# Giving each piece of a software-pipelined round its own place in the order, in a two-layer graph and attention kernel

## The chip, the cores and the metric

The kernel runs on one core of a Trainium2 chip. The metric is the device time of one execution in microseconds (us). A core has a matmul engine (TensorE, PE in profiles), a vector engine (VectorE, DVE), an activation engine (ScalarE, ACT), a general engine (GpSimd, POOL) and a synchronisation engine (SyncE, SP), which here only issues transfers. Each engine takes its instructions in the order in which the program emitted them, and semaphores hold an instruction until the data or the buffer that it needs is there.

## The reference

Inputs are `x` of 128 graphs x 128 nodes x 512 features, one 128 x 128 adjacency `adj` for all, and the weights, all float32. Two layers follow each other:

```
q, k, v = x @ Wq0.T, x @ Wk0.T, x @ Wv0.T            # layer 0
rel = adj.T * (q @ k.T)                              # per graph, 128 x 128
x   = layernorm(x + (rel / norm(rel, axis=rows)) @ v)

q, k, v = x @ Wq1 + bq, x @ Wk1 + bk, x @ Wv1 + bv   # layer 1, 8 heads of 64
w   = softmax(q @ k.T / 8 + where(adj == 0, -1e9, 0))
x   = layernorm(x + w @ v)
```

## The kernel before

**Groups and kinds of projection.** The 128 graphs go in 32 groups `g` of 4. A group needs five projections, each a product of a 512 x 512 weight with 512 tokens: `m` (layer 0, with Wq0 and Wk0 multiplied together once at the start, so that one projection takes the place of two), `v0`, and in layer 1 `q`, `k`, `v1`. Each is done by Strassen's scheme in its variant with few additions: seven products of quarters in place of eight. Three of the seven (1, 6, 7) are done whole (`whole`); the other four (2 to 5) are each split again by the same scheme (`inner`), two for either half of the tokens, and their seven small products are added up in pairs. Sums of weight blocks are made once at the start; sums of token blocks are made in each group by `token_sums` and `inner_token_sums` (L271 to L311), mostly on POOL.

**Pieces.** A `Projection` is cut into pieces that are emitted one at a time. `inner(th, n)`, for two token halves `th` and `n` of 0 to 3, runs small matmuls (L446) into PSUM tiles `c` and `d`, and ACT and DVE carry them out: n = 0 a copy on ACT (L458) and an add on DVE (L459), n = 1 two copies (L464, L465), n = 2 an add (L470), n = 3 a copy (L474) and, for `th` = 1, a sum of two halves on POOL (L476). `whole(i, m)` for i of 1, 6, 7 and m of 0, 1 runs four matmul instructions (L436) into one half of a PSUM tile `a`, which is never cleared between i = 1, 6 and 7: each product is added to what is there. `add` (L483, L488, L491) reads `a` on DVE after 1 and after 6, so product 6 can't start in that half before DVE has read product 1, and product 7 not before it has read product 6. The read after 6 also needs the POOL sum of L476.

**Other pieces of a group.** In layer 0 `l0_score` does the 128 x 128 products of a graph (L542), masks them on DVE (L543) and squares them on POOL (L544); `l0_norm` sums the squares of all four graphs by a matmul (L553); `l0_out` multiplies by `v0` and adds to `x`. `x1_spill`, `x1_stage` and `x1_transpose` bring the result through DRAM into a transposed form, with its token sums; `x_transpose` does so for `x` itself. In layer 1 `attn_scores` does eight heads of a graph, masked on DVE (L130), `attn_exp` two heads' exponentials on ACT (L627), `attn_spill` writes them to DRAM (L634), `attn_stage` and `attn_transpose` fetch and transpose them (L642, L646), `attn_out` multiplies by `v1` (L659), and `attn_back`, `attn_rows`, `attn_res`, `attn_sum`, `attn_stats`, `attn_norm`, `attn_write` bring the rows back, add the residual, normalise and store.

**Shared buffers.** Most tiles have one buffer. The tile tagged `v0` holds the v0 projection of one group and, once that is used, the softmax weights of graphs 0 and 1 of an earlier group; `yT` likewise serves m, the weights of graphs 2 and 3, and the residual rows of graphs 0 and 1. PSUM has a pool of six tiles (`ps_m`) for all but the `a` tiles, which have two (`ps_a`). Streamed weights (`stream`, L193) have a ring of two.

**The order.** It is written by hand. Round r holds the projections m and v0 of group r + 1 and q, k, v1 of group r, in five slots of 7 units, so a round is R = 35 units long. Every piece has a key, and pieces are emitted by rising key. The matmul pieces of a projection sit at fixed offsets in its slot, the same for each kind: for instance (L831 and the line after it)

```
    WHOLES = ((4.17, 1, 0), (5.33, 1, 1), (6.5, 6, 0), (7.67, 6, 1), (8.83, 7, 0), (10.0, 7, 1))
    INNER = ((0, 0, 0), (1.17, 0, 1), (2.33, 0, 2), (3.5, 0, 3), (2.4, 1, 0), (3.57, 1, 1), (4.67, 1, 2), (5.83, 1, 3))
```

where an entry is (offset, i, m) or (offset, th, n). The other pieces have keys from small tables: `ZERO` for layer 0, `STEADY` for the attention of most groups, `QUICK` for the last but one and `LAST` for the last. Pieces may share a key; then the order of the calls decides. A lower-layer group is thus two rounds ahead of the attention that still drains.

Of the kernel before, what the change touches and what calls it, by code (L numbers as in the profile page):

```python
# [18 lines left out]
def kernel(  # L19
# [15 lines left out]
    nc = tc.nc  # L35
# [3 lines left out]
    G = 4  # L39
# [338 lines left out]
    class Projection:  # L378
# [10 lines left out]

        def begin(self):  # L390
            k, g = self.kind, self.g
            self.xT, self.t, u = (XT[g], TX[g], UX) if k in ("m", "v0") else (X1T[g], TX1[g], UX1)
            self.u = u.get(g)
            self.y = {}
            if k == "m":
                YT[g] = y = one.tile([P, C, G, P], F32, tag="yT", name=f"yT_{g}")
            elif k == "q":
                QT[g] = y = one.tile([P, C, G, P], F32, tag="qT" if g < NG - 1 else "yT", name=f"qT_{g}")
            elif k == "k":
                KT[g] = y = one.tile([P, C, G, P], F32, tag="kT", name=f"kT_{g}")  # L400
            elif k == "v0" or not self.late:
                y = one.tile([P, G, D], F32, tag="v0", name=f"{k}_{g}")
                (V0 if k == "v0" else V1)[g] = self.y = {h: y[:, 2 * h:2 * h + 2] for h in range(2)}
            else:
                V1[g] = self.y = {0: one.tile([P, 2, D], F32, tag="v10", name=f"v1_{g}_0")}
                self.s = one.tile([P, 2, 2, HF], F32, tag="rel", name=f"s_{self.name}")
            if not self.wide:
                self.y = {h: y[:, :, 2 * h:2 * h + 2] for h in range(2)}

        def out(self, eh, th):  # L410

# [264 lines left out]
        nc.sync.dma_start(o, OD.pop((g, b)).rearrange("p f d -> p (f d)"))  # L676
        SOFT[g, b] = o, SOFT[g, b][1]

    def attn_res(g, b):
        xr = room(g, b, 1)  # L680
        nc.sync.dma_start(xr, X1D[g, b // 2][b % 2])
        SOFT[g, b] = SOFT[g, b][0], xr, SOFT[g, b][1]

    def attn_sum(g, b):

        o, xr, rs = SOFT[g, b]
        f = o.rearrange("p (f r) -> p f r", r=Q)
        nc.vector.tensor_tensor(f, f, rs.rearrange("p s y a -> p (s y a)")[:, :, None].to_broadcast([P, A * H // 2, Q]),
                                op=ALU.mult)
# [103 lines left out]
    def last_store(g, b):  # L793
# [4 lines left out]


    R = 35  # L800
    dense, short = {}, {}

    ZERO = (
        ((18, 19, 20, 21), 22, (36, 36, 37, 37), 38, (39, 40), (40, 41), (42, 43), (46, 47, 49, 49)),
        ((11.5, 11.5, 11.75, 12.5), 13.75, (19.5, 21.5, 22.5, 18.5), 23.5, (26, 28), (29, 29.5), (30, 31.5), (37.5, 38.5, 41, 44.5)),
        ((11.5, 12.5, 11.75, 12.5), 13.75, (18.5, 19.5, 21, 22), 23, (24, 25), (25, 26), (26, 28), (31, 32, 33, 34)),
    )
    STEADY = (  # L810
        (32.75, (32.5, 34.5, 35, 35, 35), (35, 36.5), 41.5, (44, 49, 51.5, 56, 60, 64.5, 68, 68)),
        (32.75, (35.5, 38.5, 38.5, 41.5, 41.5), (41.5, 41.5), 42, (47.5, 49, 51, 52, 60, 65, 69, 69)),
        (49, (49.5, 49.5, 50.5, 50.5, 52.5), (55, 55), 57.5, (58.5, 67.75, 67.75, 70, 73, 75, 77, 77)),
        (49, (50.5, 55, 55, 55, 55), (56.5, 56.5), 60.5, (63.5, 67.75, 69, 74.5, 76, 82, 83, 85.5)),
    )
    QUICK = (
        (32.75, (32, 33.5, 34.5, 34.5, 35), (35, 38), 40.5, (41, 43, 43.5, 47.5, 48.5, 50.5, 50.5, 50.5)),
        (36, (37, 37, 37, 37, 37), (39.5, 40.5), 41.5, (44.5, 45.5, 47.5, 50, 52, 53, 55, 62)),
        (37, (37.5, 41, 41, 41, 41), (41, 41), 45.5, (47.5, 50, 57.5, 57.5, 57.5, 59, 59.5, 63)),
        (37, (39, 41.5, 42.5, 44, 47), (44, 47), 49.5, (51, 52, 57.5, 61, 61, 64.5, 68.5, 68.5)),  # L820
    )
    LAST = (
        (18, (18, 18), (20, 22), (25.25, 25.5), 29, 35, 37.5),
        (18, (18, 19.5), (24, 24.5), (28, 31), 40, 45.5, 46),
        (19.5, (20, 23.5), (28.5, 29), (31, 37), 41, 51, 51),
        (23, (23.5, 27), (29.5, 32), (33.5, 41.5), 51, 53, 54.5),
    )


    PLAIN = ((0, 1), (1, 5), (3, 6), (4, 2), (5, 3), (6, 7), (9, 4))  # L830
    WHOLES = ((4.17, 1, 0), (5.33, 1, 1), (6.5, 6, 0), (7.67, 6, 1), (8.83, 7, 0), (10.0, 7, 1))  # L831
    INNER = ((0, 0, 0), (1.17, 0, 1), (2.33, 0, 2), (3.5, 0, 3), (2.4, 1, 0), (3.57, 1, 1), (4.67, 1, 2), (5.83, 1, 3))

    RES = 59

    def at(r, k, f, *a):
        short.setdefault(R * r + k, []).append((f, a))

    for r in range(-1, NG):
        todo = [("m", r + 1), ("v0", r + 1)] if r < NG - 1 else []  # L840
        if r < 0:
            todo.reverse()
        todo += [("q", r), ("k", r), ("v1", r)]
        for j, (kind, g) in enumerate(todo):
            if not 0 <= g < NG:
                continue
            pr = Projection(kind, g)
            if pr.plain:
                for k, i in PLAIN:
                    dense[R * r + 7 * j + k] = pr.step, (i,)  # L850
                continue
            for k, f, *a in (*((k, pr.whole, i, m) for k, i, m in WHOLES), *((k, pr.inner, th, n) for k, th, n in INNER)):
                assert R * r + 7 * j + k not in dense
                dense[R * r + 7 * j + k] = f, a
            if g or kind not in ("m", "v0"):
                if not (g == 1 and kind in ("m", "v0")):
                    at(r, 7 * j - 7.5, stream, kind, g)
    halves = [(dh, h) for dh in range(2) for h in range(2)]
    for g in range(NG):

        for h in range(2):
            if g:
                at(g - 2, 12, load_staged, g, h)
                at(g - 1, 12 + 4 * h, load, g, h)
        last = g == NG - 1

        sc, no, ou, de, ln, sp, st, tr = ZERO[0 if g == 0 else 2 if last else 1]
        for h in range(2):
            at(g - 1, sp[h], x1_spill, g, h)
            at(g - 1, st[h], x1_stage, g, h)  # L870
        for i, (dh, h) in enumerate(halves):
            if g or i:
                at(g - 2, ((25.5, 27, 28.5, 30) if g != 1 else (22, 23, 24, 25))[i], x_transpose, g, dh, h)
            at(g - 1, tr[i], x1_transpose, g, dh, h)
        for b in range(G):
            at(g - 1, sc[b], l0_score, g, b)
            at(g - 1, ou[b], l0_out, g, b)
            at(g - 1, ln[b // 2], l0_layernorm, g, b)
        at(g - 1, no, l0_norm, g)
        at(g - 1, de, l0_rstd, g)  # L880

        if last:
            at(g, 2, last_residual, g)
        for b in range(G):
            if last:
                sc, e, t, o, st, no, w = LAST[b]
                at(g, sc, last_scores, g, b)
                for i in range(2):
                    at(g, e[i], last_exp, g, b, i)
                    at(g, t[i], last_transpose, g, b, i)  # L890
                    at(g, o[i], last_out, g, b, i)
                at(g, st, last_stats, g, b)
                at(g, no, last_norm, g, b)
                at(g, w, last_store, g, b)
                continue
            s, ex, sp, st, pk = QUICK[b] if g == NG - 2 else STEADY[b]
            at(g, s, attn_scores, g, b)
            for i in range(4):
                at(g, ex[i + 1], attn_exp, g, b, 2 * i)
            for i in range(2):  # L900
                at(g, sp[i], attn_spill, g, b, i)
            at(g, st, attn_stage, g, b)
            pieces = attn_transpose, attn_out, attn_back, attn_rows, attn_sum, attn_stats, attn_norm, attn_write
            for k, f in zip(pk, pieces):
                at(g, k, f, g, b)
                if f is attn_rows:
                    at(g, RES if g < NG - 2 and b < 2 else k, attn_res, g, b)

    at(-1, 8, masks)
    V1S = ((one, "v10"), (one, "v11"))  # L910
    WTS = ((one, "wl"), (two, "wT"))
    at(-1, 41, layer1_weights, "k", "k", V1S)
    at(-1, 41, streamed_sums, "k", nc.gpsimd)
    for k, name, eng in ((38.5, "v0", nc.vector), (17, "m", nc.vector), (28, "q", nc.gpsimd), (49.5, "k", nc.gpsimd),
                         (52, "v1", nc.gpsimd)):
        at(-1, k, resident_sums, name, eng)
        if name in ("m", "v0"):
            at(-1, k, streamed_sums, name, eng)

    with tc.manual_schedule():  # L920
        layer0_weights()
        for k in sorted({*short, *dense}):
            if k == -R:
                weight_sums(whole_weights("m"), m21, nc.vector)
                for name, key, stage in (("v", "v1", V1S), ("q", "q", WTS)):
                    layer1_weights(name, key, stage)
                    streamed_sums(key, nc.gpsimd)
            for f, a in short.get(k, ()):
                f(*a)
            if k in dense:  # L930
                f, a = dense[k]
                f(*a)


# [27 lines left out]
```

## Time and profile before

Three runs took 3173.1, 3183.88 and 3184.35 us; the median is 3183.88. The profiled execution spans 3181.8 us.

| engine | busy us | share of the span |
|---|---|---|
| PE (matmuls) | 2638.7 | 83% |
| PEld (weight loads, beside the matmuls) | 2262.9 | 71% |
| DVE | 1927.3 | 61% |
| POOL | 1467.6 | 46% |
| ACT | 1020.3 | 32% |

The mean granted clock of TensorE is 0.933. The queues moved 553 MB, 174 GB/s over the span, and the transfers kept the DMA engines busy for 60% of it. Between the first and the last 100 us the profile repeats itself every 99 us or so, once per group. A row of waits names the waiting instruction, its engine and line, then what it waited for, the sum in us, how many times, and the longest. A row of a stretch gives its bounds and length, then the busy time of each engine with the number of its instructions.

### The profile page before, as it was taken

What the parts mean: (1) busy time and instruction counts of PE and PEld (TensorE: products, weight loads), DVE (VectorE), ACT (ScalarE), POOL (GpSimd) and SP (SyncE); (2) the same over time, 40 slices, a digit from 0 to 9 for tenths busy, and PEclk for the clock granted to TensorE, in tenths of its full rate; (3) what the DMA queues carried; (4) which work ended last, traced back from release to release, by engine and by line L of the source; (5) the groups of instructions that cost most, each with busy time, mean ns of one, the idle gap of its engine ahead of it and who ended that gap; (6) DMA issues with size and microseconds to landing.
All of it is one profiled execution on the core that took longest, in us unless ns stands there. A gap on an engine that the chain in (4) does not pass through costs nothing. (4 is left out here: it accounts for less than half of the span.)

```text
span 3181.8 us, 54401 instructions
## 1 busy us (share of the span) xinstructions
PE 2638.7 (83%) x18456; PEld 2262.9 (71%) x18456; DVE 1927.3 (61%) x5440; ACT 1020.3 (32%) x3598; POOL 1467.6 (46%) x1958
## 2 busy tenths in 40 slices
PE   7888888888888888888888888888888888888887
PEld 5677677777777677677767777777767767776776
DVE  5555566656666556665566665566655666555666
ACT  1233333233332333333323323233233333332334
POOL 5534544445444345444454443545434544445444
PEclk9999999999999999999999999899999999999999
DMA  6555666666656666656666665665565665666654
GB/s 158 152 152 168 193 181 174 176 173 178 188 168 172 177 171 186 189 159 174 174 186 185 179 172 170 173 190 174 166 176 169 187 189 160 181 171 182 185 171 127
DMA packets 532248, 553.29 MB, mean 174 GB/s; under 512 B 40192, under 2 KB 427392, under 8 KB 531968
## 3 DMA queue, kind: packets, MB, share of 16 engines
q1 hardware_dynamic: 531968, 549.81, 60.4%
q8 instruction: 145, 2.38, 0.3%
q14 instruction: 135, 1.11, 0.1%
HBM read 380.44 MB, written 169.21 MB: 173 GB/s over the span
## 5 line engine op out<-in xcount | busy, mean ns | idle before, releaser
L627 ACT ACTIVATE w<-w,nmax 128x128 f32<-128x128 f32 x992 | 384.8, 392 | 3.9 <-DVE nmax L130 3.9
L436 PE MATMUL pa_v<-wc_v,tx 128*128 128x256 f32 x1024 | 270.4, 387 | 61.6 <-DVE v L491 61.5
L446 PE MATMUL pc_v<-wd_v,ux 128*128 128x128 f32 x756 | 176.0, 320 | 144.4 <-ACT v L458 144.4
L476 POOL TENSOR_TENSOR qT<-qT 128x512 f32<-128x512 f32 x32 | 40.6, 1269 | 523.0 <-ACT qT L474 523.0
L446 PEld LDWEIGHTS pc_v<-wd_v,ux 128*128 128x128 f32 x756 | 143.6, 223 | 174.6 <-ACT v L458 156.4
L130 DVE CUSTOM_DVE_ANT_0 w<-ps,mask 128x128 f32<-128x128 f32 x1024 | 221.4, 286 | 32.7 <-PE ps L607 31.1
L436 PEld LDWEIGHTS pa_v<-wc_v,tx 128*128 128x128 f32 x1024 | 175.3, 191 | 87.7 <-DVE v L491 73.8
L436 PE MATMUL pa_m<-tx,wc_m 128*128 128x256 f32 x512 | 164.2, 452 | 57.1 <-DVE yT L491 56.3
L279 POOL TENSOR_TENSOR tx<-x1T,tx 128x512 f32<-128x512 f32 x32 | 40.7, 1273 | 362.9 <-DVE tx L278 362.9
L567 POOL TENSOR_SCALAR ve<-st 128x1 f32<-128x1 f32 (+1 forms) x157 | 57.2, 364 | 300.0 <-DVE st L563 292.0
L690 POOL TENSOR_TENSOR xr<-xr,bv_b 128x512 f32<-128x512 f32 x58 | 73.8, 1272 | 262.8 <-DMA xr<-x1d 126.2
L627 ACT ACTIVATION_READ_ACCUMULATOR w<-w,nmax 128x1 f32 x992 | 189.3, 191 | 0.0
L491 DVE TENSOR_TENSOR v<-pa_v,v 128x256 f32<-128x256 f32 x190 | 79.2, 417 | 178.3 <-POOL v L476 150.6
L436 PE MATMUL pa_k<-tx,wc_k 128*128 128x256 f32 x512 | 142.8, 402 | 51.1 <-DVE kT L483 51.0
L659 PE MATMUL po<-wT,v 128*64 128x128 f32 x1984 | 167.7, 339 | 3.5 <-DVE wT L646 3.5
L659 PEld LDWEIGHTS po<-wT,v 128*64 128x64 f32 x1984 | 149.1, 176 | 19.6 <-issue 15.9
L446 PE MATMUL pc_v<-wr_v,ux 128*128 128x128 f32 x756 | 161.0, 298 | 0.0
L646 DVE STREAM_TRANSPOSE wT<-wl 128x1024 f32<-128x1024 f32 x124 | 153.5, 1238 | 12.2 <-DMA wl<-wd 9.0
L436 PEld LDWEIGHTS pa_m<-tx,wc_m 128*128 128x128 f32 x512 | 103.5, 224 | 79.4 <-DVE yT L491 68.7
L483 DVE SCALAR_TENSOR_TENSOR kT<-pa_k,bk_sb,kT 128x256 f32<-128x256 f32 x256 | 113.5, 475 | 74.3 <-POOL kT L476 68.8
L446 PE MATMUL pc_v<-wr_v,tx 128*128 128x128 f32 x756 | 154.5, 288 | 0.0
L459 DVE TENSOR_TENSOR v<-pd_v,v 128x256 f32<-128x256 f32 x95 | 40.0, 422 | 188.0 <-ACT v L458 179.9
(315 smaller groups left out, 7819.0 us busy)
## 6 DMA issues: line engine op xcount, KB each, us to landing
wd<-w SPq DMA_DIRECT2D x248, 256.0 KB, 5.2
wl<-wd SPq DMA_DIRECT2D x496, 128.0 KB, 3.7
wr_v<-wr_v SPq DMA_DIRECT2D x63, 896.0 KB, 5.1
xl_x<-in_x_dram SPq DMA_DIRECT2D x256, 128.0 KB, 4.9
x<-in_x_dram SPq DMA_DIRECT2D x64, 512.0 KB, 4.4
x1d<-x SPq DMA_DIRECT2D x64, 512.0 KB, 6.5
xl_h<-x1d SPq DMA_DIRECT2D x256, 128.0 KB, 3.0
od<-oT SPq DMA_DIRECT2D x496, 64.0 KB, 1.9
```

The source lines that it names most:

```text
L130: nc.vector.tensor_tensor_reduce(out=dst, in0=scores, in1=m, scale=-HD ** -0.5, scalar=3.0e38, op0=ALU.add, op1=ALU.min, accum_out=least)
L279: nc.gpsimd.tensor_tensor(t[:, 3], quarter(xT, 1, 0), t[:, 1], op=ALU.subtract)
L436: nc.tensor.matmul(bank[:, m, :], l[:, k, m * P:(m + 1) * P], r[:, k, :], start=start and m == 0 and k == 0, stop=(m == 1 and k == 1), ski ...
L446: nc.tensor.matmul(dst[:, n, :], l, r, start=start and n == 0, stop=True, skip_group_check=True)
L476: nc.gpsimd.tensor_tensor(self.held(0, 1), self.held(0, 1), self.held(1, 1), op=ALU.add)
L483: nc.vector.scalar_tensor_tensor(o, self.a[:, m], b1[self.kind][:, 2 * eh + m:2 * eh + m + 1], o, op0=ALU.add, op1=ALU.add)
L491: nc.vector.tensor_tensor(o[:, m], self.a[:, m], s[:, m], op=ALU.add)
L567: nc.gpsimd.tensor_scalar(ve[:, :n], stats[:, :n, 1], EPS, None, op0=ALU.add)
L627: nc.scalar.activation(w[:, s, :, a, :], w[:, s, :, a, :], AF.Exp, bias=nmax[:, i:i + 1], scale=-1.0, accum_out=sums[:, i:i + 1])
L646: nc.vector.transpose(wT, SOFT[g, b][0].rearrange("p a i r -> p i a r"))
L659: nc.tensor.matmul(p[s * HD:(s + 1) * HD, a, :], V1[g][b // 2][:, b % 2, h * HD:(h + 1) * HD], wT[:, s * (H // 2) + a].rearrange("p q t -> ...
L690: nc.gpsimd.tensor_tensor(xr, xr, bv_b, op=ALU.add)
```

## The change

The fixed offsets and the small tables go. In their place a table `KEYS` gives every piece its own key: by the name of the piece, for projections also by kind and index, for per-graph pieces by graph. A key has five values, for group 0, group 1, the groups between, the last but one and the last. Keys are now counted from 35 g for the piece's own group g: m and v0 of a group have negative ones, since they are emitted in rounds before. Thus v0's `inner(1, 0)` at -14.6 for group g + 2 is emitted where key 55.4 of group g would be. Ties are cut by the order of the calls.

What this is for: pieces of different kinds of projection no longer need the same rhythm, whole products of two projections can alternate, and each piece on ACT, DVE, POOL and SyncE can be moved among the others on its own. For this, three small things change in the pieces themselves: `begin` no longer looks up the token tiles, which may not be made yet when it runs (they become properties), `attn_res` no longer needs `attn_rows` ahead of it (its tile lives in `XR`), and the first weight sums become one piece, `start_sums`. The instructions are those of before, in another order.

The diff, cut to the code and the keys that are spoken of later (the third value is that of groups 2 to 29):

```diff
--- before.py
+++ after.py
@@ -389,8 +389,6 @@
         def begin(self):
             k, g = self.kind, self.g
-            self.xT, self.t, u = (XT[g], TX[g], UX) if k in ("m", "v0") else (X1T[g], TX1[g], UX1)
-            self.u = u.get(g)
             self.y = {}
 ...
+        @property
+        def xT(self):
+            return (XT if self.kind in ("m", "v0") else X1T)[self.g]
+
+        @property
+        def t(self):
+            return (TX if self.kind in ("m", "v0") else TX1)[self.g]
+
+        @property
+        def u(self):
+            return (UX if self.kind in ("m", "v0") else UX1)[self.g]
 ...
+    XR = {}
+
     def attn_res(g, b):
         xr = room(g, b, 1)
         nc.sync.dma_start(xr, X1D[g, b // 2][b % 2])
-        SOFT[g, b] = SOFT[g, b][0], xr, SOFT[g, b][1]
+        XR[g, b] = xr
 
     def attn_sum(g, b):
 
-        o, xr, rs = SOFT[g, b]
+        o, rs = SOFT[g, b]
+        xr = XR.pop((g, b))
         f = o.rearrange("p (f r) -> p f r", r=Q)
         nc.vector.tensor_tensor(f, f, rs.rearrange("p s y a -> p (s y a)")[:, :, None].to_broadcast([P, A * H // 2, Q]),
                                 op=ALU.mult)
@@ -798,138 +811,335 @@
 
 ...
     R = 35
-    dense, short = {}, {}
 ...
-    STEADY = (
-        (32.75, (32.5, 34.5, 35, 35, 35), (35, 36.5), 41.5, (44, 49, 51.5, 56, 60, 64.5, 68, 68)),
-        (32.75, (35.5, 38.5, 38.5, 41.5, 41.5), (41.5, 41.5), 42, (47.5, 49, 51, 52, 60, 65, 69, 69)),
-        (49, (49.5, 49.5, 50.5, 50.5, 52.5), (55, 55), 57.5, (58.5, 67.75, 67.75, 70, 73, 75, 77, 77)),
-        (49, (50.5, 55, 55, 55, 55), (56.5, 56.5), 60.5, (63.5, 67.75, 69, 74.5, 76, 82, 83, 85.5)),
-    )
 ...
-    PLAIN = ((0, 1), (1, 5), (3, 6), (4, 2), (5, 3), (6, 7), (9, 4))
-    WHOLES = ((4.17, 1, 0), (5.33, 1, 1), (6.5, 6, 0), (7.67, 6, 1), (8.83, 7, 0), (10.0, 7, 1))
-    INNER = ((0, 0, 0), (1.17, 0, 1), (2.33, 0, 2), (3.5, 0, 3), (2.4, 1, 0), (3.57, 1, 1), (4.67, 1, 2), (5.83, 1, 3))
 ...
-    for r in range(-1, NG):
-        todo = [("m", r + 1), ("v0", r + 1)] if r < NG - 1 else []
-        if r < 0:
-            todo.reverse()
-        todo += [("q", r), ("k", r), ("v1", r)]
-        for j, (kind, g) in enumerate(todo):
-            if not 0 <= g < NG:
-                continue
+    KEYS = {
 ...
+    KEYS = {
+        ("inner", "k", 0, 0): (33.9, 26.7, 31.7, 34.3, 21.3),
+        ("inner", "k", 0, 1): (34.7, 28.4, 34.6, 35.7, 22),
+        ("inner", "k", 0, 2): (36, 30.6, 35.74, 37.9, 22.8),
+        ("inner", "k", 0, 3): (39, 34.1, 37.5, 39.8, 23.9),
+        ("inner", "k", 1, 0): (37, 27.9, 33.04, 35.6, 21.9),
+        ("inner", "k", 1, 1): (38.2, 29.3, 33.9, 35.8, 22.7),
+        ("inner", "k", 1, 2): (38.5, 30.7, 35.7, 38.8, 23),
+        ("inner", "k", 1, 3): (39.8, 33.2, 37.1, 40, 24),
+        ("inner", "m", 0, 0): (None, -48, -24.4, -25.1, -24.6),
+        ("inner", "m", 0, 1): (None, -44, -22.46, -21.7, -23),
+        ("inner", "m", 0, 2): (None, -40, -20.83, -20, -21.47),
+        ("inner", "m", 0, 3): (None, -31.2, -19, -16.2, -19.8),
+        ("inner", "m", 1, 0): (None, -43, -23, -23, -24.5),
+        ("inner", "m", 1, 1): (None, -39.4, -21.8, -21.8, -21.8),
+        ("inner", "m", 1, 2): (None, -32, -20.2, -20.3, -21),
+        ("inner", "m", 1, 3): (None, -30, -18.3, -14.4, -18),
+        ("inner", "q", 0, 0): (25.2, 32.3, 27.73, 27.2, 11.2),
+        ("inner", "q", 0, 1): (28.7, 32.6, 28.24, 33.4, 13.2),
+        ("inner", "q", 0, 2): (30.3, 37, 31.6, 35.46, 16),
+        ("inner", "q", 0, 3): (32.3, 38, 32.6, 36, 25.3),
+        ("inner", "q", 1, 0): (27.9, 34.7, 27.9, 27.7, 13),
+        ("inner", "q", 1, 1): (29.5, 35.97, 29.31, 29.64, 15.97),
+        ("inner", "q", 1, 2): (31, 37.7, 31, 31.7, 20.5),
+        ("inner", "q", 1, 3): (32.1, 38.7, 32.3, 35.5, 26.3),
+        ("inner", "v0", 0, 0): (None, -46, -14.9, -14.1, -16.2),
+        ("inner", "v0", 0, 1): (None, -31.4, -13.2, -12.9, -13.2),
+        ("inner", "v0", 0, 2): (None, -27, -12.2, -12.5, -11),
+        ("inner", "v0", 0, 3): (None, -24.3, -12, -11.4, -10),
+        ("inner", "v0", 1, 0): (None, -39, -14.6, -14.01, -13.8),
+        ("inner", "v0", 1, 1): (None, -32.6, -13.07, -12.6, -12.7),
+        ("inner", "v0", 1, 2): (None, -26, -12.11, -12, -10.9),
+        ("inner", "v0", 1, 3): (None, -22, -11, -11.3, -10.5),
 ...
+        ("whole", "k", 1, 0): (38, 34, 35.8, 38.09, 23.8),
+        ("whole", "k", 1, 1): (39.2, 35, 37.9, 40.05, 26.5),
+        ("whole", "k", 6, 0): (40.6, 38.1, 40.6, 42.5, 30),
+        ("whole", "k", 6, 1): (42, 40.9, 42.3, 44.1, 35),
+        ("whole", "k", 7, 0): (44, 42, 43.4, 45.11, 35.6),
+        ("whole", "k", 7, 1): (44.1, 43, 44, 45.3, 38),
+        ("whole", "m", 1, 0): (None, -39.3, -19.76, -19, -21.4),
+        ("whole", "m", 1, 1): (None, -28, -17.6, -14.2, -19),
+        ("whole", "m", 6, 0): (None, -25.9, -16.4, -14, -17),
+        ("whole", "m", 6, 1): (None, -23, -14, -11.63, -14),
+        ("whole", "m", 7, 0): (None, -16.6, -12.8, -11, -12.9),
+        ("whole", "m", 7, 1): (None, -13.2, -12.02, -10, -11.7),
+        ("whole", "q", 1, 0): (31.1, 37.4, 33.2, 37, 18),
+        ("whole", "q", 1, 1): (38.4, 39.1, 35.6, 38.4, 27.5),
+        ("whole", "q", 6, 0): (41, 39.8, 37.6, 39.82, 33),
+        ("whole", "q", 6, 1): (42.7, 41.3, 40, 41, 35.5),
+        ("whole", "q", 7, 0): (44.5, 44.1, 42.6, 44, 41),
+        ("whole", "q", 7, 1): (45, 44.5, 43.2, 45.1, 42.3),
+        ("whole", "v0", 1, 0): (None, -24, -10.3, -10.5, -9.99),
+        ("whole", "v0", 1, 1): (None, -18, -9.66, -9.8, -9.5),
+        ("whole", "v0", 6, 0): (None, -16, -8.9, -8.6, -8),
+        ("whole", "v0", 6, 1): (None, -14, -7.28, -7.4, -7.7),
+        ("whole", "v0", 7, 0): (None, -13.14, -6.58, -6.5, -5.4),
+        ("whole", "v0", 7, 1): (None, -8, -5.68, -4.06, -5.37),
+        ("whole", "v1", 1, 0): (46.7, 46.5, 44.05, 46.7, 56.6),
+        ("whole", "v1", 1, 1): (47.7, 48.5, 46.2, 46.9, 60),
+        ("whole", "v1", 6, 0): (49, 50.7, 47.6, 49.2, 64.4),
+        ("whole", "v1", 6, 1): (50.2, 52.8, 49.4, 51.9, 67.2),
+        ("whole", "v1", 7, 0): (50.85, 54, 52.56, 54, 72),
+        ("whole", "v1", 7, 1): (53, 54.6, 53.4, 56, 73),
 ...
+        ("attn_exp", 0, 0): (47.5, 46, 46, 49, None),
+        ("attn_exp", 0, 2): (46.6, 47.4, 44.98, 50, None),
+        ("attn_exp", 0, 4): (47.3, 50.6, 47.4, 55.9, None),
+        ("attn_exp", 0, 6): (48, 49, 46.74, 54.3, None),
+        ("attn_exp", 1, 0): (48.5, 46.1, 48, 50.6, None),
+        ("attn_exp", 1, 2): (49.5, 50.9, 48.5, 51.83, None),
+        ("attn_exp", 1, 4): (50.8, 49.2, 48.25, 52, None),
+        ("attn_exp", 1, 6): (50, 50.8, 49.5, 52.6, None),
 ...
+        ("attn_scores", 0): (45.8, 44.9, 44.6, 46.702, None),
+        ("attn_scores", 1): (48.4, 45, 46.8, 49.5, None),
+        ("attn_scores", 2): (61, 61.5, 61.65, 53.3, None),
+        ("attn_scores", 3): (61.4, 62, 62.1, 46, None),
+        ("attn_spill", 0, 0): (50.84, 48, 50.3, 52.4, None),
+        ("attn_spill", 0, 1): (50.87, 51.6, 52.5, 58.3, None),
+        ("attn_spill", 1, 0): (50.9, 52, 54, 52.55, None),
+        ("attn_spill", 1, 1): (51.3, 52.7, 55.2, 56.1, None),
 ...
+        ("attn_stage", 0): (53.2, 53, 55.3, 62, None),
+        ("attn_stage", 1): (57.9, 59.2, 58.4, 60.8, None),
 ...
+        ("attn_sum", 0): (74.23, 72.7, 73, 97.7, None),
+        ("attn_sum", 1): (72.8, 75.2, 72.72, 99.6, None),
 ...
+        ("l0_norm",): (-19, -3, -4.5, -4.1, -5.3),
 ...
+        ("l0_score", 0): (-38, -12.4, -10, -9.7, -10.8),
+        ("l0_score", 1): (-33, -10, -9.8, -8.9, -8.5),
+        ("l0_score", 2): (-22, -9, -9.83, -8.7, -10.6),
+        ("l0_score", 3): (-24, -11, -9.2, -8.5, -9.8),
 ...
+        ("stream", "v0"): (None, None, -21.3, -22.5, -22.9),
 ...
+        ("x1_transpose", 1, 1): (20, 22.7, 24.4, 24.7, 9.3),
 ...
+    }
+
+    todo = []
+
+    def at(f, g, a, n):
+        keys = KEYS[n]
+        k = keys[0] if g is None else R * g + keys[0 if g == 0 else 1 if g == 1 else 4 if g == NG - 1 else 3 if g == NG - 2 else 2]
+        todo.append((k, len(todo), f, a))
+
+    def each(f, g, *a):
 ...
+    pairs = [(d, h) for d in range(2) for h in range(2)]
+    for g in range(NG):
+        for kind in KINDS:
             pr = Projection(kind, g)
             if pr.plain:
-                for k, i in PLAIN:
-                    dense[R * r + 7 * j + k] = pr.step, (i,)
+                for i in range(1, 8):
+                    at(pr.step, g, (i,), ("step", kind, i))
                 continue
-            for k, f, *a in (*((k, pr.whole, i, m) for k, i, m in WHOLES), *((k, pr.inner, th, n) for k, th, n in INNER)):
-                assert R * r + 7 * j + k not in dense
-                dense[R * r + 7 * j + k] = f, a
-            if g or kind not in ("m", "v0"):
-                if not (g == 1 and kind in ("m", "v0")):
-                    at(r, 7 * j - 7.5, stream, kind, g)
-    halves = [(dh, h) for dh in range(2) for h in range(2)]
 ...
     with tc.manual_schedule():
         layer0_weights()
-        for k in sorted({*short, *dense}):
-            if k == -R:
-                weight_sums(whole_weights("m"), m21, nc.vector)
-                for name, key, stage in (("v", "v1", V1S), ("q", "q", WTS)):
-                    layer1_weights(name, key, stage)
-                    streamed_sums(key, nc.gpsimd)
-            for f, a in short.get(k, ()):
-                f(*a)
-            if k in dense:
-                f, a = dense[k]
-                f(*a)
+        for _, _, f, a in sorted(todo, key=lambda t: t[:2]):
+            f(*a)
```

## The prediction

> **What bounds the kernel now.** I first read busy time and clock by rounds of 99 us. Columns: stretch, its length, busy us of PE, PEld, DVE, ACT, POOL, granted clock, DMA share, GB/s.
>
> ```profile
> 505.00:604.00 99.00, 83.18 (x579) 71.64 (x579) 60.09 (x170) 31.76 (x112) 45.22 (x60) 0.91 0.62 175
> 1594.00:1693.00 99.00, 82.67 (x585) 71.17 (x586) 61.25 (x172) 31.64 (x112) 45.05 (x60) 0.93 0.62 178
> ```
>
> Every round looks alike: PE 82.5 of 99 us, DVE 60, POOL 45, ACT 32. PE is the bound, and 16.5 us of each round (543 us of 3181.8) it stands still. Next, the waits in total, PE's rows: us, times, longest.
>
> ```profile
> PE pc_v L446 <- ACT v L458: 144.4, 30, 6.7
> PE pn L553 <- POOL sq L544: 104.9, 31, 3.5
> PE pa_k L436 <- DVE kT L483: 88.3, 89, 2.0
> PE pa_v L436 <- DVE v L491: 70.6, 64, 8.1
> PE pa_m L436 <- DVE yT L491: 61.8, 73, 2.0
> PE pa_q L436 <- DVE qT L483: 13.7, 31, 1.3
> ```
>
> Three kinds make nearly all of it. Over 30 like rounds: the v0 projection's second piece waits 4.8 us, the norm's matmul 3.5 us, and the whole products (L436, idle by the groups' rows 238 us) some 7.9 us in pieces of about one; 0.4 us is left. Then I cut one round at its two long stops:
>
> ```profile
> 1641.00:1646.30 5.30, 0.77 (x5) 0.34 (x3) 0.04 (x1) 0.37 (x1) 1.61 (x2) 0.72 0.86 237
> 1646.30:1651.00 4.70, 4.70 (x21) 4.34 (x22) 1.87 (x3) 0.65 (x2) 0.00 (x0) 0.59 0.32 92
> 1661.60:1665.20 3.60, 0.13 (x5) 0.07 (x8) 0.00 (x0) 0.44 (x1) 3.28 (x10) 0.81 0.77 255
> 1665.20:1672.00 6.80, 6.80 (x73) 5.97 (x73) 3.22 (x15) 0.38 (x1) 2.14 (x2) 0.60 0.20 61
> 1672.00:1700.00 28.00, 25.68 (x158) 21.17 (x159) 20.54 (x61) 12.65 (x49) 5.54 (x7) 1.00 0.60 179
> ```
>
> After each long stop the clock is 0.59 to 0.60 for 4.7 and 6.8 us, and 1.00 elsewhere, through stops of 1.5 us as well. So the two long stops cost a second time: 4.7 x 0.41 + 6.8 x 0.40 = 4.65 us of PE per round.
>
> The causes are in the timeline of the same round (ACT, then SyncE's queue, then POOL; start, us, brackets: idle before):
>
> ```profile
> 1645.86 0.37 ACT L458 COPY v<-pc_v 128x256 f32<-128x256 f32 x1 [6.11 <-DMA wd<-w]
> ...
> 1637.34 2.27 SPq L642 DMA_DIRECT2D wl<-wd  x4
> 1639.65 1.21 SPq L634 DMA_DIRECT2D wd<-w  x2
> ...
> 1653.91 1.27 POOL L279 TENSOR_TENSOR tx<-x1T,tx 128x512 f32<-128x512 f32 x1 [11.22 <-DVE tx L278]
> ...
> 1660.85 1.26 POOL L285 TENSOR_TENSOR tx<-x1T 128x512 f32<-128x512 f32 x1
> 1662.08 1.11 POOL L544 TENSOR_TENSOR sq<-rel 128x128 f32<-128x128 f32 x3
> ```
>
> The v0 tile holds the softmax weights of graphs 0 and 1 before. Its first copy waits until their spill has landed; the spill's exponentials end at 1638.8, it is issued at 1639.65 behind a staging load, and the copy starts 6.2 us later. The norm's matmul needs the four squares, and these stand on POOL behind a set of token sums that runs from 1653.9 to 1662.1.
>
> [...] stops of 4.53 and 3.47 us are followed by a clock near 0.6, those of 1.5 us are not. [...] a ready square waits behind sums it doesn't need. So an order alone can take time away or add it.
>
> **The change part by part.** No instruction is added or removed, so all cost is in waits. I sorted the old and the new keys of one steady round and summed PE's work between a producer and its consumer. PE's prices, from starts in the timeline at clock 1.00: 0.89 us for an inner piece (0.45 for its last), 0.88 for a whole piece, 0.89 for one l0_score, 0.86 l0_out, 1.0 for one attn_scores, 0.95 attn_out, 0.6 the norm. A round is 73.0 us of it. This is counting of work, not a time.
>
> *v0 against the spill.* Before: after graph 1's last exponentials (key 41.5) come whole m 6,0, inner v0 0,0 and whole m 6,1, 2.65 us, then the piece that needs the copy. After: the last exponential is at 49.5, the copy for graph 1's half at 55.4 and the piece that needs it at 56.93; eleven pieces more lie between, 9.7 us. The trace's need from the end of the exponentials is 7.0 us. From graph 1's scores on it is 15.2 us of PE work against masking 3.0 (8 x (0.286 + 0.083)), exponentials 4.7 (8 x (0.392 + 0.191)), copies between 2.2, spill 6.2, together 16.1. So it is nearly hidden: 4.8 becomes 1.0 (bounds 0 and 4.8).
>
> *The norm.* Before: 1.3 us of PE work between the last l0_score and l0_norm. After (50.8 to 55.5 in the attention group's keys): 11.0 us, of whole v0 and inner q pieces, two scores and two attn_out; and 16.3 us from the transpose that starts the token sums, against 1.4 us of DVE and 11.2 us of POOL (1653.9 to the last square's end at 1665.1). Hidden: 3.5 becomes 0 (bounds 0, 1).
>
> *Whole products.* A whole piece adds onto the PSUM half which DVE must have read after the one before. Before: 2.2 to 2.7 us of PE work between 1,0 and 6,0 for every kind, and the read of 6 also waits for POOL's sum (L476), which before is emitted just ahead of it: "DVE v L491" waits 150.6 us for it. After: 3.5 us for m, 4.4 for v0, 5.6 v1, 7.0 k, 7.1 q, since two projections are interleaved; inner 1,3 to whole 6,0 of v0 goes from 0 to 5.3 us, of k to 5.8, of m to 2.6. The chain needs copy 0.37 + POOL 1.27 + add 0.42 = 2.1 us and its queueing. DVE's load, summed by the rows per 5 to 6 us of PE work, had peaks of 7.6 and 7.5 us before and 6.4 us at most after. I take 7.9 to 3.0 (bounds 1.0 and 7.9).
>
> *New waits.* At the head of m, an exponential of graph 0 now stands on ACT ahead of m's first copy, and waits for DVE's masks; PE has 3.7 us until it needs the copy, against up to 4.5. Behind it the queue holds m's other copies and all exponentials. In the middle, scores of graphs 2 and 3 and both q starts ask for eight banks of six within 3 us, while DVE masks 5.9 us in order. Attention rows have 10.6 us of PE work until DVE sums them, some 6 us of issue and waiting plus 5.4 us landing; if late, all of DVE's queue waits. No row of before shows these; bounds 0 and 6, I take 2.5.
>
> Streams, x loads and token sums have 4 to 12 us of PE work before their first use, against landings of 4.4 to 5.6 us, mostly requested earlier: nothing. SyncE's waits are mere place in its queue. Prologue and last group have their own columns; I count no gain there.
>
> Sum: idle 1.0 + 0 + 3.0 + 2.5 + 0.4 = 6.9 instead of 16.6 us, -9.7. Half-clock loss: [...] it goes from 4.65 to 0.7 (bounds 0, 3), -4.0. Together -13.7 us in each of 30 rounds, -411: 3184 - 411 = 2773, say **2770 us**.
>
> **Rivals.** *Nearly all waits go*: only 1.4 us idle and no half clock, -19.8 x 30: 2590. For it: PE work of 73.0 us leaves room, DVE would be 60 of about 79. Against: DVE, ACT and POOL stay FIFO.
>
> *The spill wait stays*, because the graph 1 spill now is one place ahead of the copy that waits for it, and ACT comes late to the exponentials: 4.8 us and its half clock (1.9) stay. -(16.6 - 10.7) - 2.7 = -8.6, x 30: 2926.
>
> *DVE lags*: at 60 us of a shorter round, in-order waits for rows or masks delay the adds; whole waits stay at 7.9, new waits reach 6. -1.3 - 3.0 = -4.3, x 30: 3055.
>
> *Slower*: finely mixed queues block each other (SyncE holds a spill behind a staging load that waits for a transpose that waits for a copy), 3 us per round more than saved: 3270. For it: every queue is in order, and two projections open leave fewer banks. Against: in the list I found no producer that comes later relative to its consumer by more than its need.
>
> **How the numbers follow.** Forecast 0.60, nearly all 0.12, spill stays 0.11, DVE lags 0.10, slower 0.07. The range from 2630 to 2990 takes the forecast's bounds and the spill case; half of the nearly-all case and the last two are out, some 0.2. Within 0.5% is only an accident between the last two: 0.02; faster 0.92, slower 0.06.
>
> **What would show it.** Right: the mean clock rises from 0.933 to about 0.99; PE's share to 90% or more; "pn L553" leaves PE's waits; "pc_v <- ACT v" falls under 45 us; DVE's wait for POOL v L476 falls under 60; PE's waits on L436 total 100 us or less. Wrong: [...] many PE waits for DVE masks (bank reuse) or ACT copies of m that sum to over 150 us.

## The result: 2475 us, 0.779 of the time before

The changed kernel takes 2475.08 us (median of 4 runs, 2470.28 to 2483.81) against 3180.14 us for the kernel before on the same chip (four runs; the table above has three of them). The ratio is 0.7788, with a 95% interval of 0.776 to 0.7816. The forecast was 2770 us with a range of 2630 to 2990: the direction was right, the size was not. It gained 705 us where 414 were forecast, and lies 155 us under the range. It even goes past the rival "nearly all waits go", which was put at 2590.

The engines' row of the changed kernel's page:

```profile
PE 2421.0 (98%) x18456; PEld 2147.3 (87%) x18456; DVE 1969.6 (80%) x5440; ACT 1031.8 (42%) x3598; POOL 1464.7 (59%) x1958
```

PE stands still for 2471.9 - 2421.0 = 50.9 us, where it stood 543.1. It also is busy 217.7 us less with the same 18456 instructions. The mean clock rose from 0.933 to 0.997. The same view by stretches, now of 77 us, which is about a round; one in the middle of the run:

```profile
1242.00:1319.00 77.00, 76.59 (x589) 68.33 (x588) 60.88 (x169) 33.95 (x117) 46.26 (x61) 1.00 0.81 221
```

DVE, ACT and POOL do per round about what they did, in 77 instead of 99 us, and the clock is full throughout. Of PE's waits, the largest are now these (with the new line numbers: L456 are the inner matmuls, L446 the whole ones, L480 the inner add of n = 2, L486 POOL's sum, L501 the whole add):

```profile
PE pc_m L456 <- DVE yT L480: 12.2, 22, 0.9
PE pa_v L446 <- DVE v L501: 9.5, 15, 1.5
PE po L669 <- DVE wT L656: 6.8, 8, 2.2
```

Neither the v0 wait for the spill nor the norm's wait for the squares is in the list, and the whole products wait some 10 us in all where they waited 238.

### The profile page after: what moved, and what is told of

The parts are those of the page before. It is cut to its first block, busy times and chain, and to the rows that moved or that the text cites. A ratio compares the mean times of both kernels' runs of the same rounds, so it can differ in the third digit from the quotient of the medians.

```text
span 2471.9 us, 54459 instructions
## 1 busy us (share of the span) xinstructions
PE 2421.0 (98%) x18456; PEld 2147.3 (87%) x18456; DVE 1969.6 (80%) x5440; ACT 1031.8 (42%) x3598; POOL 1464.7 (59%) x1958
## 4 chain that ended last, share of the span: by engine, by line
PE 72%; DMA 13%; DVE 5%; SPq 4%; POOL 3%; issue 2%; ACT 0%; DVEq 0%; POOLq 0%
PE pa_v L446 11%; PE pc_v L456 9%; PE pc_q L456 7%; DMA wl<-wd 7%; PE pc_k L456 5%; PE pa_k L446 5%; PE pa_q L446 5%; PE ps L617 4%; PE po L669 4%; PE pa_m L446 4%; PE po L597 4%; PE pc_m L456 4%; PE pst L552 3%; DMA wd<-w 3%; DMA xl_h<-x1d 2%
## 5 line engine op out<-in xcount | busy, mean ns | idle before, releaser
L446 PE MATMUL pa_v<-wc_v,tx 128*128 128x256 f32 x1024 | 264.6, 386 | 9.3 <-DVE v L501 9.0
L446 PEld LDWEIGHTS pa_v<-wc_v,tx 128*128 128x128 f32 x1024 | 180.1, 191 | 35.0 <-DVE v L501 13.7
L567 POOL TENSOR_TENSOR rn<-ss,mhalf 128x4 f32<-128x4 f32 x32 | 33.0, 1031 | 207.6 <-DVE ss L565 207.6
L456 PE MATMUL pc_v<-wd_v,ux 128*128 128x128 f32 x756 | 146.3, 275 | 0.1
L456 PE MATMUL pc_v<-wr_v,tx 128*128 128x128 f32 x756 | 146.2, 275 | 0.0
L456 PE MATMUL pc_v<-wr_v,ux 128*128 128x128 f32 x756 | 146.2, 275 | 0.0
L701 DVE TENSOR_TENSOR o<-o,rs 128x512 f32<-128x512 f32 x118 | 126.4, 1075 | 23.3 <-DMA o<-od 23.2
L617 PEld LDWEIGHTS ps<-kT,qT 64*128 64x128 f32 x1984 | 118.2, 187 | 30.1 <-issue 19.9
L669 PE MATMUL po<-wT,v 128*64 128x128 f32 x1984 | 135.7, 279 | 7.1 <-DVE wT L656 6.8
L617 PE MATMUL ps<-kT,qT 64*128 64x128 f32 x1984 | 136.5, 282 | 0.0
L446 PE MATMUL pa_k<-tx,wc_k 128*128 128x256 f32 x512 | 134.2, 386 | 0.3 <-DVE kT L493 0.3
L446 PE MATMUL pa_q<-tx,wc_q 128*128 128x256 f32 x512 | 134.3, 385 | 0.1
L446 PE MATMUL pa_m<-tx,wc_m 128*128 128x256 f32 x512 | 131.4, 380 | 0.0
L669 PEld LDWEIGHTS po<-wT,v 128*64 128x64 f32 x1984 | 106.1, 136 | 29.1 <-issue 14.2
L456 PEld LDWEIGHTS pc_v<-wd_v,ux 128*128 128x128 f32 x756 | 124.3, 191 | 7.4 <-ACT s_v L475 0.5
L552 PEld LDWEIGHTS pst<-yT,xT 128*128 128x128 f32 x1024 | 125.0, 193 | 3.3
L597 PE MATMUL po<-v,rel 128*128 128x512 f32 x256 | 125.6, 594 | 0.0
```

Source lines behind the costliest of these rows:

```text
L446: nc.tensor.matmul(bank[:, m, :], l[:, k, m * P:(m + 1) * P], r[:, k, :], start=start and m == 0 and k == 0, stop=(m == 1 and k == 1), ski ...
L456: nc.tensor.matmul(dst[:, n, :], l, r, start=start and n == 0, stop=True, skip_group_check=True)
L552: nc.tensor.matmul(p, XT[g][:, dc, b, :], YT[g][:, dc, b, :], start=(dc == 0), stop=(dc == C - 1))
L567: nc.gpsimd.tensor_tensor(RN[g], ss[:, :, 0], mhalf, op=ALU.pow)
L597: nc.tensor.matmul(p, REL[g][0][:, b, :], V0[g][b // 2][:, b % 2, :], start=True, stop=True)
L617: nc.tensor.matmul(p[s][:, :, a, :], QT[g][r, a, b, :], KT[g][r, a, b, :], start=True, stop=True)
```

## The experiments

Unless another round is named, edits concern the groups of the steady state, and the lines below are those of the profiled execution. Experiments 1, 2, 3 and 9 start from the kernel before, the others from the changed one. Every ratio is to the kernel before, which was timed again beside the experiments and took 3175 to 3181 us.

**e1: the norm alone, later in the kernel before.**

```diff
-        ((11.5, 11.5, 11.75, 12.5), 13.75, (19.5, 21.5, 22.5, 18.5), ...
+        ((11.5, 11.5, 11.75, 12.5), 14, (19.5, 21.5, 22.5, 18.5), ...
```

> The kernel before with one key changed: the norm's matmul of groups 1 to 30 at 14 instead of 13.75, so that two attn_out and two attn_scores (3.9 us of PE work) come ahead of it. Theory (a stop costs its length and the half clock after it): the 3.5 us stop at pn goes and with it 2.7 us of half clock, 6.2 x 30 = 186, about 2995 us[...]. Rival (the wait moves on, since DVE's second output transpose now waits for the squares' buffer, and the masks of two score pieces stand behind it): 60 or less of it is kept, 3120 or more.

Measured: 3149 us, ratio 0.9898 (0.9866 to 0.9931). The rival was right: the wait moved.

```profile
PE pn L553 <- DVE rs L664: 57.5, 29, 2.4
PE pc_q L446 <- DVE oT L662: 24.0, 29, 0.8
```

The norm no longer waits for squares but for a PSUM bank that DVE has yet to read, and then q waits for the next. Two stops of 2.0 and 0.8 us close together take the place of one of 3.5, and the clock stays at 0.934.

**e2: the spill ahead of the staging, in the kernel before.**

```diff
-        (32.75, (35.5, 38.5, 38.5, 41.5, 41.5), (41.5, 41.5), 42, ...
+        (32.75, (35.5, 38.5, 38.5, 38.6, 38.6), (40.9, 40.9), 42, ...
```

> The kernel before with the last four exponentials of graph 1 at 38.6 instead of 41.5 and its spill at 40.9, ahead of graph 0's staging, in groups 0 to 29. Theory: v0's 4.8 us stop shrinks to 1 us or less and its half clock (1.9 us) goes, 5.7 to 6.7 x 30 = 170 to 200, about 2985 to 3015 us. Rival (ACT is the bound at m's head: earlier exponentials hold up m's copies by as much): PE waits for ACT copies of m grow to 3 us a round and the time stays over 3100.

Measured: 3001 us, ratio 0.9431 (0.9398 to 0.9464). The theory holds: "pc_v <- ACT v" leaves PE's list of waits, and the busy time of PE falls from 2638.7 to 2580.3. The 180 us are the 144.4 of the wait and the 58.4 of PE time, less some 23 us that come back: 13.8 as a new wait of the same v0 pieces for DVE (L470), and 9.3 more at the norm. Waits for ACT copies of m stay at 6.3 us in all.

**e3: both edits.**

> The kernel before with both edits. Theory: both stops and all half clock go, 12 x 30 = 360 to 390, about 2800 to 2825 us with a mean clock of 0.99; what is left to the changed kernel's 2475, some 330 us, is then the price of the short waits at the whole products and of restarts. Rival (short waits only fill the room that long stops gave DVE, so that they grow once these are gone): 2900 or more, with PE's waits on whole products over 300 us.

Measured: 2967 us, ratio 0.9327 (0.9301 to 0.9353). The time is the rival's, but not for its reason: waits on whole products are 221 us, no more than before. It is again the norm, which waits 66.5 us for DVE as in e1. DVE's timeline of one round of e3 shows what holds the bank:

```profile
1547.76 0.25 DVE L543 TENSOR_TENSOR rel<-pst,adj_sb 128x128 f32<-128x128 f32 x1
1553.34 0.42 DVE L491 TENSOR_TENSOR v<-pa_v,v 128x256 f32<-128x256 f32 x1 [5.34 <-POOL v L476]
1553.68 0.71 DVE L662 STREAM_TRANSPOSE oT<-po 128x512 f32<-128x512 f32 x1
```

DVE stands 5.34 us at a whole add of v0, which waits for POOL's sum L476; the output transpose that would free the bank is queued behind it. And POOL is late because some 8.2 us of token sums stand ahead of that sum. In the round of the kernel before that the prediction shows, the sums run from 1653.91 to 1662.1, then come the squares, and only then v0's sum:

```profile
1665.03 1.27 POOL L476 TENSOR_TENSOR v<-v 128x512 f32<-128x512 f32 x1
```

So the forecast's cause of the norm's stop, token sums ahead of the squares, was half of it: the same sums also hold v0's add, and moving the norm a little only changes which of the two PE meets.

**e9: the token sums earlier, the norm where it was.** One more key on top of e2, for the transpose of x1 that starts the sums:

```diff
-        ... (37.5, 38.5, 41, 44.5)),
+        ... (37.5, 38.5, 41, 42.9)),
```

> The kernel before with graph 1's exponentials and spill early as in the run that took v0's stop away (3001 us), and with the last transpose of x1, which starts the 8.4 us of token sums on POOL, at 42.9 instead of 44.5; the norm stays where it was. Theory (the norm's stop is POOL's backlog: the sums must be done before the squares and before v0's sum L476 come up; moving the norm alone only let the same backlog stop PE through DVE): the stop goes with its half clock, 114 + 66 = 180 us less, about 2820 us, mean clock 0.99 or more, PE's waits on whole products near 235 us still. Rival (the norm stands too close to the last score whatever POOL does): a stop of over 1.5 us at pn stays, 2930 or more.

Measured: 2828 us, ratio 0.8909 (0.8894 to 0.8924), as the theory had it. The norm's wait falls from 104.9 to 8.1 us, the clock rises to 0.989, and what is left is the short waits:

```profile
PE pa_k L436 <- DVE kT L483: 89.6, 90, 2.2
PE pa_v L436 <- DVE v L491: 71.2, 64, 8.7
PE pa_m L436 <- DVE yT L491: 57.4, 67, 2.2
...
PE pn L553 <- POOL sq L544: 8.1, 29, 1.3
```

So e2's edit and this one, in the old table, give 347 us (from 3175 beside it), half of what the change gives. The order on POOL is as before here, sums, squares, v0's sum; they only start earlier.

**e12: the same backlog put back into the changed kernel.** One key, which swaps two neighbours: the last transpose of x1 and v0's `inner(1, 3)`.

```diff
-        ("x1_transpose", 1, 1): (20, 22.7, 24.4, 24.7, 9.3),
+        ("x1_transpose", 1, 1): (20, 22.7, 23.95, 24.7, 9.3),
```

> The changed kernel with one key changed: the last transpose of x1 at 23.95 instead of 24.4 in groups 2 to 29, one place ahead of v0's inner 1,3, so that on POOL the 8.4 us of token sums come ahead of v0's sum L486. Nothing else changes its place. Theory (the kernel before stood at this place in POOL's queue: v0's add on DVE waits for POOL, and all of DVE's queue, the masks and PSUM's banks with it): DVE waits about 5 us for that sum in each round and PE stops for 3 to 5 us with half clock after it, +110 to +190, about 2590 to 2660 us. Rival (PE has enough else to do until v0's next whole products): under 2500 us.

Measured: 2615 us, ratio to before 0.8232 (0.8199 to 0.8265); 140 us more than the changed kernel, inside the theory's bounds. DVE's wait, which the changed kernel doesn't have, is back to within 2 us of the 150.6 that the kernel before had, and PE's with it:

```profile
DVE v L501 <- POOL v L486: 148.9, 28, 5.8
```
```profile
PE pa_v L446 <- DVE v L501: 99.6, 42, 3.7
```

POOL's timelines show the two orders. The changed kernel, then e12:

```profile
1285.20 1.27 POOL L486 TENSOR_TENSOR v<-v 128x512 f32<-128x512 f32 x1 [3.89 <-ACT v L484]
1287.10 1.27 POOL L279 TENSOR_TENSOR tx<-x1T,tx 128x512 f32<-128x512 f32 x1 [0.63 <-DVE tx L278]
```
```profile
1360.49 1.27 POOL L279 TENSOR_TENSOR tx<-x1T,tx 128x512 f32<-128x512 f32 x1 [5.34 <-DVE tx L278]
...
1368.65 1.27 POOL L486 TENSOR_TENSOR v<-v 128x512 f32<-128x512 f32 x1
```

v0's sum of 1.27 us starts ahead of the block of sums in the one and 8.2 us after the block's start in the other. The stop comes at v0's whole products and not at the norm, which stands late here.

**e4: the norm right behind the last score, in the changed kernel.**

```diff
-        ("l0_norm",): (-19, -3, -4.5, -4.1, -5.3),
+        ("l0_norm",): (-19, -3, -9.1, -4.1, -5.3),
```

> The changed kernel with one key changed: the norm's matmul of groups 2 to 29 at -9.1 instead of -4.5, right behind the last l0_score. In the changed kernel's trace the last square ends 6.8 us after that place. Theory (PE is the bound and nothing gives back what it loses): a stop of 6.8 us and 1.7 to 3 us of half clock in each of 28 rounds, +240 to +275, about 2715 to 2750 us, mean clock about 0.96. Rival (the stop alone, no half clock): 2665. Rival (a slack elsewhere takes it up): under 2600.

Measured: 2716 us, ratio 0.8537 (0.8509 to 0.8565), 241 us more than the changed kernel. Nothing gives the stop back:

```profile
PE pn L563 <- POOL sq L554: 186.2, 29, 7.3
```

PE's busy time grows by 63.8 us, to 2484.8, and the clock falls to 0.955. A stop of 6.4 us thus costs 2.2 us more in the work after it. So the norm's late place is needed in the changed kernel, since its squares still stand behind the token sums:

```profile
1294.05 1.27 POOL L285 TENSOR_TENSOR tx<-x1T 128x512 f32<-128x512 f32 x1
1295.28 1.47 POOL L554 TENSOR_TENSOR sq<-rel 128x128 f32<-128x128 f32 x4
```

**e11: graph 1's exponentials late and its spill behind the staging, in the changed kernel.**

```diff
-        ("attn_exp", 1, 4): (50.8, 49.2, 48.25, 52, None),
-        ("attn_exp", 1, 6): (50, 50.8, 49.5, 52.6, None),
+        ("attn_exp", 1, 4): (50.8, 49.2, 53.0, 52, None),
+        ("attn_exp", 1, 6): (50, 50.8, 53.1, 52.6, None),
-        ("attn_stage", 0): (53.2, 53, 55.3, 62, None),
+        ("attn_stage", 0): (53.2, 53, 53.9, 62, None),
```

> The changed kernel with graph 1's last four exponentials at 53 instead of 48 and 49.5, and graph 0's staging at 53.9, ahead of graph 1's spill, in groups 2 to 29. PE has 5.3 us of work from there to v0's piece that needs the copy, against exponentials 1.6, staging 1.7 and up to 6.2 from the spill's issue. Theory: a stop of some 4 us comes back at v0 and with it about 2 us of half clock and restart; 6 x 28 = 170, about 2645 us. Rival (with single spills landing in 3.6 us in the changed kernel the stop stays near 1 to 2 us): under 2560 us.

Measured: 2580 us, ratio 0.8125 (0.8091 to 0.8159), 105 us more, between the two expectations. The wait is back, but shorter than expected:

```profile
PE pc_v L456 <- ACT v L468: 70.0, 28, 3.9
```

It is 2.5 us a round, with 43.5 us of PE's busy time on top. So the place of the exponentials and of the spill against the staging is what took v0's stop away; e2 and e11 move both together, so they are not told apart. That the stop is short because spills land sooner (a median of 3.6 us in the changed kernel, 5.2 before) fits, but was not tested. A version with graph 1's exponentials and both its spills moved behind the staging (keys 54.65 to 54.85) gave no time: its order is a deadlock.

**e5: q's and k's whole products in turn, not alternating,** in the same twelve places of the changed kernel. The edit in short, third value of each key:

```diff
-  whole q 6,0 37.6   6,1 40    7,0 42.6  7,1 43.2   whole k 1,0 35.8  1,1 37.9  6,0 40.6  6,1 42.3
+  whole q 6,0 35.8   6,1 37.6  7,0 37.9  7,1 40     whole k 1,0 40.6  1,1 42.3  6,0 42.6  6,1 43.2
```

> The changed kernel with the twelve places of q's and k's whole products in groups 2 to 29 kept, but filled first by all of q and then by all of k, so that the products of one tile come 0.9 to 1.8 us of other PE work apart for k, in place of 3 to 7 us. Theory (distance between two products of one PSUM half is what took the short waits away): PE waits again at k's products 6,1, 7,0 and 7,1, about 1.2 us each, 0.5 us at q's, and some 0.25 us of restart at each, 4 to 5 us a round, +110 to +140, about 2585 to 2615 us; the clock stays at 0.99. Rival (DVE's evener load took them away, distance matters little): under 2510 us.

Measured: 2536 us, ratio 0.7986 (0.7972 to 0.7999), 61 us more. Distance matters, for half of what was expected:

```profile
PE pa_q L446 <- DVE qT L493: 39.9, 28, 4.3
PE pa_k L446 <- DVE kT L493: 35.6, 57, 2.1
```

k stops twice a round for 0.6 us and not three times for 1.2, and q once for 1.4. PE's busy time grows by 19.5 us.

**e8 and e10: two tries at the 12 us that are left at m.** e8 moves two of the attention sums on DVE and POOL behind m's add:

```diff
-        ("attn_sum", 2): (82.1, 83.65, 83.1, 118, None),
-        ("attn_sum", 3): (88.2, 88.8, 83.8, 74.8, None),
+        ("attn_sum", 2): (82.1, 83.65, 84.85, 118, None),
+        ("attn_sum", 3): (88.2, 88.8, 86.75, 74.8, None),
```

> The changed kernel with attn_sum of graphs 2 and 3 at 84.85 and 86.75 instead of 83.1 and 83.8 in groups 2 to 29, so that DVE no longer waits for rows and POOL ahead of m's add L480, at which PE waits 12 us in all. Theory: these 12 us go and nothing comes, 2463 us (0.5% less). Rival (POOL's sum of m and the stores come later and cost as much): same or up to 10 us more.

Measured: 2557 us, ratio 0.8054 (0.8038 to 0.8069), 82 us more. The wait at L480 goes, and a larger one comes at the next add behind the moved sums:

```profile
PE pa_m L446 <- DVE yT L501: 60.3, 27, 2.4
```

e10 moves only the first transpose of x1:

```diff
-        ("x1_transpose", 0, 0): (12.3, 17, 14.3, 12.2, 7.98),
+        ("x1_transpose", 0, 0): (12.3, 17, 14.85, 12.2, 7.98),
```

> The changed kernel with one key changed: the first transpose of x1 at 14.85 instead of 14.3 in groups 2 to 29, so that on DVE it comes behind m's add L480 at which PE waits 12 us in all, in place of ahead of it. Theory: DVE's order is the cause, 12 us of waits and a few of restarts go, about 2460 us. Rival (the add still comes late, behind the rows' multiplication that waits for its transfer, or what is moved back stops something else as in the run that moved the sums): 2475 us or more.

Measured: 2482 us, ratio 0.7809 (0.7787 to 0.7832), against 0.7788 for the changed kernel with an interval that overlaps: no gain. The wait at L480 falls only from 12.2 to 7.0 us and 4.5 us come at L501. No version beat the changed kernel.

## Why the prediction was wrong in size

**What bounds the kernel, and what kind of gain.** Right. PE was the bound, and its stops with what they cost beyond their length were the room; e4 shows that a stop put back is lost in full.

**The sum, term by term.** Per round, over 30 rounds, from the two lists of waits and the two busy times:

| term | forecast | measured | from |
|---|---|---|---|
| v0 against the spill | -3.8 | -4.8 | 144.4 us to none |
| norm | -3.5 | -3.5 | 104.9 us to none |
| whole products | -4.9 | -7.6 | 238 us to 10 |
| new waits, and the rest | +2.5 | -0.5 | 56 us to 41 |
| half clock, measured as all of PE's busy time | -4.0 | -7.3 | 2638.7 to 2421.0 |
| sum | -13.7 | -23.7 | 710 us of span |

Every term has the right sign but one. Three are mis-sized by about 3 us each and v0's by one, all the same way: these make the error.

*"New waits: bounds 0 and 6, I take 2.5"* is the step that failed outright. The mechanism exists, but hardly reaches PE. In the changed kernel's waits over all engines the first row is

```profile
ACT w L637 <- DVE nmax L130: 308.5, 59, 9.9
```

so ACT does stand 10 us a round waiting for masks; in the round shown, 2.3 us of it come at m's head, with m's copies queued behind. The round's timeline shows why PE doesn't care (ACT, then PE, then DVE):

```profile
1261.34 0.40 ACT L637 ACTIVATE w<-w,nmax 128x128 f32<-128x128 f32 x1 [2.33 <-DVE nmax L130]
...
1261.74 0.39 ACT L637 ACTIVATE w<-w,nmax 128x128 f32<-128x128 f32 x1
...
1262.12 0.35 ACT L468 COPY yT<-pc_m 128x256 f32<-128x256 f32 x1
```
```profile
1264.52 0.39 PE L456 MATMUL pc_m<-ux,wd_m 128*128 128x128 f32 x2
```
```profile
1260.58 0.29 DVE L130 CUSTOM_DVE_ANT_0 w<-ps,mask 128x128 f32<-128x128 f32 x1 [0.40 <-PE ps L617]
1260.80 0.08 DVE L130 DVE_READ_ACCUMULATOR2_ANT nmax<- 128x1 f32 x1
1260.80 0.29 DVE L130 CUSTOM_DVE_ANT_0 w<-ps,mask 128x128 f32<-128x128 f32 x1
```

m's first copy is done at 1262.5, two us before PE needs it. The prediction had priced masks at 0.286 + 0.083 us and exponentials at 0.392 + 0.191 by adding the mean of an instruction to that of its accumulator read. But these overlap: masks follow each other every 0.21 us here and in the kernel before, exponentials every 0.39. Eight masks take 1.7 us and not 3.0, eight exponentials 3.1 and not 4.7. With that, the 16.1 us that the v0 chain was said to need become 13.2 (1.7 + 3.1 + 2.2 + 6.2), less than the 15.2 of PE work that covers it: by this count there is no residual of 1.0, and none was measured. As for the six PSUM banks, PE's list has no wait of q's start for one, which fits masks of 1.7 us. Late attention rows do reach PE, but as no more than the 12.2 us at L480: this wait went when e8 moved the sums that use the rows.

*"I take 7.9 to 3.0"* for the whole products. The distances had been worked out as 3.5 to 7.1 us against a chain of 2.1 us, and a residual of 3.0 was then put on top for "queueing" with no row behind it. Measured is 0.3. e5 shows that distance is a cause for q and k, but not how much of the 7.6 us it makes for all kinds; DVE's evener load, the rival in e5, may have a share. POOL's backlog is not their cause: in e9 most of it is gone (DVE's wait for v0's sum falls from 150.6 to 54.4 us) and PE's waits on whole products are still 232 us.

*"Half-clock loss ... -4.0"* was near what was measured for the two long stops, after which the granted clock reads 0.50 in the round of the prediction (1646.3 to 1648.0 and 1665.2 to 1668.0 us), but beside it the prediction held that "all cost is in waits", and so left a term out. Taking away the two long stops cut PE's busy time by 58.4 us (v0's, e2) and a further 67.3 us (the norm's, e9: 2580.3 to 2513.0), together 4.2 us a round. Another 92 us went with the short stops, from e9's 2513.0 to 2421.0, while the clock rose only from 0.989 to 0.997. The timelines of the kernel before and of the changed one show one way:

```profile
1607.32 1.13 PE L436 MATMUL pa_k<-tx,wc_k 128*128 128x256 f32 x4 [1.32 <-DVE kT L483]
1608.28 0.38 PE L446 MATMUL pc_v<-wd_v,ux 128*128 128x128 f32 x2
```
```profile
1241.97 1.03 PE L446 MATMUL pa_q<-tx,wc_q 128*128 128x256 f32 x4
1242.83 1.03 PE L446 MATMUL pa_k<-x1T,wc_k 128*128 128x256 f32 x4
```

After a stop the four matmuls of a whole piece are followed by the next start 0.96 us later, in an unbroken run of such pieces 0.86 us. It is 0.96 or 0.97 after stops of 0.17 and 0.42 us in the same round too, and once without a stop, behind an `attn_out` (1245.70 to 1246.67 in the changed kernel). An estimate of how the 92 us divide: by the mean clocks, 0.011 of e9's 2826 us are lost and 0.003 of 2472, so at most 24 us are clock; the other 68 us or more fall on the stops that went, from 383 to 55 in the two lists of PE's waits, which makes 0.2 us for each beyond its length. That was never priced, though the prediction's own figures left room for it: 82.5 us of PE busy time less 4.65 of half clock is 77.9 us a round, and its pieces came to 73.0.

**The norm.** The wait went, as forecast, and the 11 us of PE work put ahead of the norm are needed for it: without them e4 has a stop of 6.4 us. What the prediction had wrong is that this is enough. It knew of "DVE v L491 <- POOL v L476: 150.6", but put it to the whole products and not to the same block of token sums. With that block ahead of v0's sum, a norm moved later meets the backlog through DVE (e1 and e3), and even with the norm late PE stops at v0's whole products (e12). An earlier block takes both waits down with the norm left in place (e9). The changed kernel needs both, the late norm and v0's sum ahead of the block.

**Two slips in the working.** The keys "50.8 to 55.5" of the norm should read 60.8 to 65.5; the pieces counted are those of the latter, and 11.0 us is right. The 7.0 us of k between 1,0 and 6,0 come to 6.3 at the prices given. Neither changes the forecast.

**The rivals.** "Nearly all waits go" was the case, at a chance of 0.12; its 2590 was too slow by 115 us, most of which is the missing term of 92 us. "The spill stays" and "DVE lags" did not happen: DVE is busy 80% of the span and PE waits for it some 35 us. The range left the true case out because its lower end took in only a part of the first rival, and that rival lacked the restarts itself.

**What would show it.** The forecast's signs (clock, PE's share, the vanished waits) all came, more strongly than named; none of the signs against came.

## What to carry to other kernels

Where one engine was the bound and each wait was covered by more work than its chain needs, a residual of zero came closer here than one put on for caution, which is a forecast like any other. Price what a stop costs beyond its length too, short stops included. Take an engine's cost of a burst from start to start in the timeline, not from the sum of mean durations. And before moving the instruction that waits, look for the long block on an in-order engine that its producer stands behind, and for what else stands behind it: in the kernel before, moving the waiting matmul alone was worth 31 us; with the block out of v0's way its place is worth 241 (e4), and one swap of two neighbours in POOL's queue 140 (e12).

## What the runs showed of the hardware

In the round of the kernel before that the prediction shows, the clock is 0.59 over the 4.7 us after a stop of 4.53 us and 0.60 over the 6.8 us after one of 3.47. In e8 a shorter stop, of 2.26 us, ends at 1312.3, and the clock is 0.76 over the next 6.7 us:

```profile
1312.30:1319.00 6.70, 6.70 (x38) 6.24 (x39) 3.32 (x6) 2.48 (x7) 1.69 (x3) 0.76 0.58 184
```

In one round of e11 a stop of 1.75 us is followed by a clock of 1.00 over the next 6.8 us. What decides whether the clock falls was not tested by a run.

The multiplication of attention rows on DVE (L688 before, L701 after) took 696 ns on average before and 1075 ns after, with the same shape, while the statistics of `x` of the same size stayed at 695 (L562, L572). Of 95 of them in the changed kernel's trace, between 200 and 2300 us, 53 took over 0.9 us, 1.47 on average, and all 53 ran beside a 128x512 sum of POOL (L703, L705), for 0.36 us or more; the other 42 took 0.69 us on average, and 22 of them met such a sum for some of that time. Whether POOL is what slows them was not tested by a run.
